# A recommendation network over 200 history items: the loop unrolled, 128-row weights in the head's second layer, three history tiles per l fetched by address

## The chip, the cores and the metric

The kernel runs on one core of a Trainium2 chip. The core's engines run side by side, each through its own list of instructions: TensorE (PE) multiplies matrices, VectorE (DVE) and ScalarE (ACT) work elementwise, GpSimd (POOL) here only starts indirect DMAs, and SyncE (SP) only starts other DMAs. They wait for one another by semaphores. ACT too can start DMAs from its own queue. The metric is the device time of one execution in microseconds (us); lower is better. Times of several runs are given as a median.

## The reference

For each of B = 16384 samples the network looks up a user, an item and a category row, and L = 200 history items. All rows have D = 64 floats. A small attention layer scores each history item against the sample's item, and the history rows are summed with these weights:

```python
u, it, c, h = u_emb[user], i_emb[item], c_emb[cate], i_emb[hist]
feat = concatenate([h, it, h - it, h * it], axis=-1)
a = dice(feat @ au_W1 + au_b1, au_alpha, axis=1)   # statistics over the batch, for each l
w = a @ au_W2 + au_b2
cur = sum(w * h, axis=0)                           # over l
z = concatenate([u, it, c, cur], axis=-1)
z = dice(z @ W1 + b1, alpha1, axis=0)
z = dice(z @ W2 + b2, alpha2, axis=0)
return z @ W3 + b3
# dice(x) = x * (p + alpha * (1 - p)), p = sigmoid((x - mean) * rsqrt(var + 1e-8))
```

The attention layer has 36 hidden values, the three layers of the head 80, 40 and 2. Everything is float32. The bulk of the data is the 200 x 16384 history rows of 256 bytes each, picked at random from a table of some 100,000 rows.

## The kernel before

The batch is cut into 128 tiles of 128 samples, and 16 tiles make a chunk; so each history position l has ND = 8 chunks, and the body is 200 x 8 = 1600 steps of one chunk each. A step k handles several chunks at different stages (lines 421 to 445): it gathers chunk k, turns and multiplies chunk k - 1, adds and measures k - 3, and applies the gate and the weighted sum of chunk k - 10 (LAG), for which the statistics of its whole l must be known. There are 16 row buffers, so gathers may run up to six steps ahead of the weighted sum that frees a buffer.

`fetch` (line 346) starts one indirect DMA on POOL per tile: 128 rows by a list of indices on the partitions. `turn` transposes the rows on DVE and copies the result on ACT; `product` multiplies on PE, with the item's transposed chunk loaded from memory by SP (`load_items`, line 393, three buffers; the load for step k + 1 is issued in step k and waits until DVE's product of k - 2 has read that buffer). `gate` runs on ACT, `weights` and `weigh` on DVE. `moments` closes the statistics of an l in one step of eight.

Some tiles are not gathered by POOL. For the chunks in SIDES, the last tile may come "by address": SP loads the 128 indices into one partition (`addr`), DVE scales them to byte addresses, and then SP or ACT loads them into registers in groups (`TENSOR_LOAD`, line 303) and starts one plain DMA of 256 bytes per row into a `side` or `aside` buffer (lines 314 and 325). In `turn`, ACT copies that buffer into the chunk's rows (line 389). Before, the pattern has a period of four l: SP brings three tiles and ACT two in four l, that is 1.25 of 128 tiles per l. Class `Queue` decides in which step each group is fetched: `when(q)` gives the step, and `lead` and `span` shift and spread it. In a step SP's rows stand ahead of its item load, and ACT's rows stand behind the gate.

The order of all instructions on each engine is the order in which the program writes them. The 192 first l run in a device loop of two turns with 96 l each (lines 503 to 506); the last 8 l and the head follow. Ahead of it, the opening (lines 465 to 501) loads index lists, prepares the attention weights, gathers and turns the items, fills the first addresses, and loads the head's weights.

The head (from line 508) gathers category and user rows for each chunk, runs layer one while the last steps of the body drain, takes the statistics over the batch (`head_moments`: statistics, a small matmul that sums over partitions, deviation, a second matmul, root, reciprocal), and runs layers two and three. Layer one's 80 outputs are split: 64 per half of the samples in `za`, 16 in `zb`, whose four chunks lie on 32 partitions each. Layer two therefore multiplies each half chunk twice, once with the 128-row weights `w2a` and once with the 32-row slice `w2b[q]`:

```python
nc.tensor.matmul(pz[c % 4][:, cols], w2a, cur[c][:, cols], start=True, stop=False)
nc.tensor.matmul(pz[c % 4][:, cols], w2b[q], ab[c // 4][q, cols], start=False, stop=True)
```

A float32 matmul appears in the profile as two passes.

Of the kernel before, what the change touches and what calls it, by code (L numbers as in the profile page):

```python
# [20 lines left out]
LPB = 96  # L21
# [6 lines left out]
SIDES = (5, 6)  # L28
PERIOD = 4
BY_SP = ((1, 5), (2, 5), (3, 5))  # L30
BY_ACT = ((1, 6), (3, 6))
# [5 lines left out]
def din_kernel(  # L37
# [36 lines left out]
    BODY = L - L % LPB if L > LPB else 0  # L74
# [79 lines left out]
    def transpose(dst, of):  # L154
        for i in range(2):
            for e in range(2):
                nc.vector.transpose(by_tile(dst[ts(e, D)], i), of[ts(i, D), :, ts(e, S)])  # L157
# [58 lines left out]
    w2b = make("w2b", P, P)  # L216
# [4 lines left out]
    res = [make(f"res{i}", P, 4, TD, ZO) for i in range(2)]  # L221
# [7 lines left out]
    def head_weights():  # L229
# [8 lines left out]
        for g in range(2):  # L238
# [6 lines left out]
            for j in range(4):  # L245
                r = slice(j * S + g * ZB, j * S + (g + 1) * ZB)
                nc.sync.dma_start(w2b[r, g * ZA : g * ZA + Z2], W2[ZA:])
# [14 lines left out]
    class Queue:  # L262


        def __init__(self, engine, tiles, group, lead, span, buffers, addresses):
            self.engine, self.tiles, self.group, self.lead, self.span = engine, tiles, group, lead, span
            self.buffers, self.addresses, self.n = buffers, addresses, len(buffers)
            self.per = P // group

# [12 lines left out]
        def events(self, k, count):  # L282
            for m in range(count):
                q = m * self.per
                if self.when(q) - 8 == k:
                    yield self.load, m
                if self.when(q) - 5 == k:
                    yield self.scale, m
            for q in range(count * self.per):
                if self.when(q) == k:  # L290
                    yield self.fetch, q

        def load(self, m, l0):
            j = NC + SIDES.index(self.tiles[m % len(self.tiles)][1])
            nc.sync.dma_start(self.addresses[m % self.n], r_hist[ds(l0 + self.line(m), 1), j * P : (j + 1) * P])

        def scale(self, m, l0):
            nc.vector.tensor_scalar_mul(self.addresses[m % self.n], self.addresses[m % self.n], ROW)

        def fetch(self, q, l0):  # L300
# [120 lines left out]
    def step(k, last=None, rows_by_scalar=()):  # L421

        def has(j):
            return last is None or j <= last

        if has(k):
            fetch(k)
# [11 lines left out]
        for q, l0 in rows_by_scalar:  # L439
            by_scalar.fetch(q, l0)  # L440
# [6 lines left out]
    def ask(k, l0, n, more):  # L447
        late = []
        for q in queues:
            per = len(q.tiles)  # L450
            for what, m in q.events(k, n * per // PERIOD + (more and 2)):
                if q is by_scalar and what == q.fetch:
                    late.append((m, l0))
                else:
                    what(m, l0)
        return late

    def steps(l0, n, more):
        for k in range(n * ND):
            l, c = divmod(k, ND)  # L460
            if c == 0 and l + 1 < n + more:
                load_hist_ids((l + 1) % IDX, l0 + l + 1, by_address(l + 1))
            step(k, rows_by_scalar=ask(k, l0, n, more))

    with tc.manual_schedule():
# [6 lines left out]
        for t in (*hT, *xs, *side, *aside, *hm):  # L472
# [3 lines left out]
        for i in range(3):  # L476
            nc.vector.memset(rstds[i], 0.0)
            nc.vector.memset(shifts[i], 0.0)
        nc.vector.bn_stats(stats[-1 % 3][:, 0, :], hm[0][:, :CH])
        for c in range(1, 2 * ND):  # L480
            nc.vector.tensor_copy(stats[-1 % 3][:, c, :], stats[-1 % 3][:, 0, :])
# [12 lines left out]
        for t in px:  # L494
            layer(t, [(blk_m, hm[0])])
        load_items(0)
        for k in range(-16, 0):
            ask(k, 0, L, 0)
        head_weights()
        for t in rows[2:]:  # L500
            nc.vector.memset(t, 0.0)
# [6 lines left out]
    K = (L - BODY) * ND  # L508
# [3 lines left out]
    zb = flat_rows[3:5]  # L512
    pz = [px[K % 2], px[(K + 1) % 2], pg, py]
# [11 lines left out]

    def head_layer(j):
        c, u = divmod(j, 2)
        if u == 0:
            pairs = ((2, ucT[j % 4]), (1, itT[(K + c) % ITEMS]))
        else:  # L530
            transpose(hT[c % TURNED], cur[c].rearrange("p (n d) -> p n d", d=D))
            pairs = ((3, hT[c % TURNED]), (0, ucT[j % 4]))
        layer(pz[0], [(w1a[:, f], t) for f, t in pairs], first=not u, last=u == 1)
        layer(pz[1][:S], [(w1b[:, f], t) for f, t in pairs], first=not u, last=u == 1)
        if u:
            nc.scalar.activation(za[c], pz[0], AF.Identity, bias=b1a)
            measure_head(0, c, za[c])
            nc.scalar.activation(zb[c // 4][ts(c % 4, S)], pz[1][:S], AF.Identity, bias=b1b)
# [3 lines left out]
    with tc.manual_schedule():  # L542
        steps(BODY, L - BODY, 0)
        for j in range(2 * ND + 2):
# [4 lines left out]
            step(K + j, last=K - 1)  # L549
            if 1 <= j <= 2 * ND:  # L550
                transpose(ucT[(j - 1) % 4], spare[(j - 1) % 3])
            if j >= 2:
                head_layer(j - 2)

        def head_moments(i, same):
            mv = small.tile([P, 2], F32, tag=f"hmv{i}", name="hmv")
            nc.vector.bn_aggr(mv, zst[i].rearrange("p c s -> p (c s)"))
            pm = (pg, py)[i % 2]
            nc.tensor.matmul(pm[:, 0:1], same, mv[:, 0:1], start=True, stop=True)
            mean = small.tile([P, 1], F32, tag=f"hmean{i}", name="hmean")  # L560
            nc.vector.tensor_copy(mean, pm[:, 0:1])
            dev = small.tile([P, 1], F32, tag=f"hdev{i}", name="hdev")
            nc.vector.tensor_sub(dev, mv[:, 0:1], mean)
            nc.vector.scalar_tensor_tensor(dev, dev, dev, mv[:, 1:2], ALU.mult, ALU.add)
            nc.tensor.matmul(pm[:, CH : CH + 1], same, dev, start=True, stop=True)  # L565
            rstd = small.tile([P, 1], F32, tag=f"hrstd{i}", name="hrstd")
            shift = small.tile([P, 1], F32, tag=f"hshift{i}", name="hshift")
            scale_and_shift(mean, pm[:, CH : CH + 1], rstd, shift)
            return rstd, shift
# [11 lines left out]
        na, nb = head_moments(0, same_a), head_moments(1, same_b)  # L581
        ab = ucT[:2]
        for j in range(2):
            dice(ab[j], zb[j], nb, al1b, alb)
        for c in range(ND + 1):
            if c < ND:
                dice(cur[c], za[c], na, al1a, ala)
                q = ts(c % 4, S)
                for h in range(2):
                    cols = ts(h, CH)  # L590
                    nc.tensor.matmul(pz[c % 4][:, cols], w2a, cur[c][:, cols], start=True, stop=False)
                    nc.tensor.matmul(pz[c % 4][:, cols], w2b[q], ab[c // 4][q, cols], start=False, stop=True)
            if c:
                nc.scalar.activation(z2[c - 1], pz[(c - 1) % 4], AF.Identity, bias=bias2)
                measure_head(2, c - 1, z2[c - 1])

        n2 = head_moments(2, same_a)
        for c in range(ND):
# [56 lines left out]
```

## Time and profile before

| | us |
|---|---|
| median of 3 runs (32289.11 to 32293.9) | 32292.97 |
| the profiled execution, its own time | 32292.57 |
| its span, first to last instruction | 32290.8 |
| POOL busy | 24281.4 |
| DVE busy | 22882.8 |
| PE busy | 9918.7 |
| ACT busy | 6057.9 |

The page gives the busy time of each engine and then groups of instructions: line, engine, operation, tiles written and read, shape and count; behind the first bar the busy time and the mean length in ns, behind the second the idle time of that engine just before the group's instructions and what ended it. "issue" means that the engine waited for nothing that the profile shows. In the timeline the first column is the start in us, the second the length. PEclk is the clock that TensorE was granted, as a share of full speed. "SPq" and "ACTq" are DMAs issued from these engines' queues.

### The profile page before, as it was taken

The page shows a single profiled execution, that of the slowest core. Times are in us where ns is not written, and L with a number is a line of the kernel's source. Part 1 is how long each engine was busy: PE and PEld are TensorE (multiplying, and loading weights), DVE is VectorE, ACT ScalarE, POOL GpSimd, SP SyncE. Part 2 cuts the span into 40 slices and gives each one's busy share as a digit, 9 for nine tenths or more (in the row PEclk, how much of TensorE's full clock was granted, in tenths as well). Part 3 has the DMA queues.
Part 4 walks back from the last instruction along what each step waited for, and adds up shares of the span by engine and source line. Part 5 has one row for each costly group of instructions (what it writes and reads, how often), then busy time and mean ns, then how long its engine had stood idle before and what let it go on. Part 6 is the DMA issues. An engine that isn't in the chain of part 4 may idle for free.

```text
span 32290.8 us, 175696 instructions
## 1 busy us (share of the span) xinstructions
PE 9918.7 (31%) x13212; PEld 3717.7 (12%) x13212; DVE 22882.8 (71%) x31911; ACT 6057.9 (19%) x5738; POOL 24281.4 (75%) x25739
## 2 busy tenths in 40 slices
PE   2333323333333333233233333333333333333334
PEld 1111111111111111111111111111111111111111
DVE  6777777777777777777677777777777777777775
ACT  1111111111111111111111111111111111111111
POOL 7777777777777777777777777777777777777776
PEclk6666666666666666666666666666666666666666
DMA  2222222222222222222222222222222222222221
GB/s 55 54 54 53 54 54 54 54 54 54 54 54 54 54 54 53 54 54 54 53 54 54 54 53 54 54 54 54 53 54 54 54 54 53 54 54 54 54 53 39
DMA packets 1179260, 1726.19 MB, mean 53 GB/s; under 512 B 559010, under 2 KB 559260, under 8 KB 1177980
## 3 DMA queue, kind: packets, MB, share of 16 engines
q0 software_dynamic: 823488, 844.90, 15.1%
q1 hardware_dynamic: 328604, 866.62, 7.8%
q14 instruction: 1175, 9.63, 0.1%
q10 hardware_dynamic: 25888, 3.33, 0.1%
q8 instruction: 105, 1.72, 0.0%
HBM read 1708.61 MB, written 4.33 MB: 53 GB/s over the span
## 4 chain that ended last, share of the span: by engine, by line
POOL 32%; issue 11%; DMA 4%; DVE 4%; ACT 1%; PE 0%; SPq 0%; DVEq 0%; POOLq 0%; ACTq 0%
POOL rows L128 32%; DMA rows<-in_L_rec_i_emb,idx 4%; DVE hT L157 1%; DVE xs L376 0%; DVE st L381 0%; DVE pg L359 0%; DVE py L358 0%; ACT L354 0%; DVE py L360 0%; DVE py L372 0%; ACT pg L354 0%; ACT pg L355 0%; DVE pg L364 0%; DVE other L408 0%; DVE mv L404 0%
## 5 line engine op out<-in xcount | busy, mean ns | idle before, releaser
L128 POOL DMA_INDIRECT rows<-in_L_rec_i_emb,idx x25350 | 23918.5, 944 | 7749.0 <-issue 7452.1
L162 PE MATMUL px<-hT,blk_h 128*128 128x512 f32 x6404 | 5972.1, 1088 | 21637.1 <-DVE xs L376 21622.7
L157 DVE STREAM_TRANSPOSE hT<-rows 64x512 f32<-64x512 f32 x6404 | 4518.4, 706 | 7674.6 <-DMA rows<-in_L_rec_i_emb,idx 7476.0
L391 ACT COPY py<-hT 128x1024 f32<-128x1024 f32 x1601 | 1627.3, 1016 | 24930.0 <-DVE hT L157 24930.0
L162 PEld LDWEIGHTS px<-hT,blk_h 128*128 128x128 f32 x6404 | 1880.6, 324 | 24758.2 <-DVE xs L376 23104.6
L162 PE MATMUL px<-hm,blk_m 128*128 128x512 f32 x6412 | 3970.5, 752 | 369.2 <-DVE hm L398 368.0
L358 DVE TENSOR_TENSOR py<-pg,xs 128x1024 f32<-128x1024 f32 x1610 | 1985.0, 1233 | 615.7 <-ACT pg L355 468.9
L162 PEld LDWEIGHTS px<-hm,blk_m 128*128 128x128 f32 x6412 | 1757.9, 277 | 3276.1 <-issue 1878.5
L381 DVE BATCH_NORM_STATS2 st<-xs 128x6 f32<-128x512 f32 x3206 | 2062.3, 685 | 55.1
L359 DVE STREAM_TRANSPOSE pg<-py 128x1024 f32<-128x1024 f32 x1610 | 2037.1, 1265 | 55.9
L360 DVE TENSOR_REDUCE py<-pg 128x32 f32<-128x1024 f32 x1610 | 1985.0, 1233 | 54.7
L372 DVE TENSOR_TENSOR py<-rows,pg 128x1024 f32<-128x1024 f32 x1610 | 1978.3, 1229 | 55.2
L373 DVE TENSOR_TENSOR cur<-py,cur 128x1024 f32<-128x1024 f32 x1610 | 1970.7, 1224 | 55.6
L376 DVE TENSOR_TENSOR xs<-px,itp 128x1024 f32<-128x1024 f32 x1603 | 1963.2, 1225 | 50.6
L354 ACT ACTIVATE pg<-xs,sh,rs 128x1024 f32<-128x1024 f32 x1610 | 1937.1, 1203 | 35.3 <-DVE py L372 32.6
L398 DVE TENSOR_TENSOR hm<-py,itT 128x1024 f32<-128x1024 f32 x1601 | 1933.9, 1208 | 0.0
L355 ACT ACTIVATE pg<-pg,au_al,au_1al 128x1024 f32<-128x1024 f32 x1610 | 1895.0, 1177 | 54.2
L364 DVE SCALAR_TENSOR_TENSOR pg<-py,au_bias,part 32x16 f32<-32x16 f32 x6440 | 1538.9, 239 | 227.0
L361 DVE COPY part<-py 64x32 f32<-64x32 f32 x1610 | 312.6, 194 | 55.9
L354 ACT ACT_TABLE_LOAD x204 | 261.7, 1283 | 3.6
L171 ACT ACT_TABLE_LOAD x203 | 260.4, 1283 | 7.5 <-PE pg L565 4.0
L408 DVE COPY other<-mv 32x2 f32<-32x2 f32 x804 | 158.6, 197 | 15.1
(138 smaller groups left out, 1514.0 us busy)
## 6 DMA issues: line engine op xcount, KB each, us to landing
itT<-items SPq DMA_DIRECT2D x1609, 512.0 KB
rows<-in_L_rec_i_emb,idx POOLq DMA_INDIRECT x25350
side<-in_L_rec_i_emb SPq DMA_DIRECT2D x19200, 0.2 KB
aside<-in_L_rec_i_emb ACTq DMA_DIRECT2D x12800, 0.2 KB
idx<-in_r_hist SPq DMA_DIRECT2D x200, 63.0 KB
items<-itT SPq DMA_DIRECT2D x8, 512.0 KB
idx<-in_r_hist SPq DMA_DIRECT2D x150, 0.5 KB
addr<-in_r_hist SPq DMA_DIRECT2D x150, 0.5 KB
```

The lines of the kernel that those rows point to most:

```text
L128: nc.gpsimd.indirect_dma_start(out=dst[:, n, :], out_offset=None, in_=table, in_offset=bass.IndirectOffsetOnAxis(ap=ids, axis=0),)
L157: nc.vector.transpose(by_tile(dst[ts(e, D)], i), of[ts(i, D), :, ts(e, S)])
L162: nc.tensor.matmul(dst[:, ts(i, CH)], lhsT, rhs[:, ts(i, CH)], start=(first and j == 0), stop=(last and j == len(pairs) - 1), skip_group_c ...
L354: nc.scalar.activation(pg, xs[k % XR], AF.Sigmoid, bias=shifts[i], scale=rstds[i])
L358: nc.vector.tensor_mul(py, pg, xs[k % XR])
L359: nc.vector.transpose(pg, py)
L360: nc.vector.reduce_sum(total, pg.rearrange("p (n a) -> p n a", a=S), axis=mybir.AxisListType.X)
L372: nc.vector.tensor_mul(of, rows[k % ROWS], w.unsqueeze(2).to_broadcast([P, TD, D]))
L373: nc.vector.tensor_add(cur[k % ND], py, cur[k % ND])
L376: nc.vector.tensor_add(xs[k % XR], px[k % 2], itp[k % ND])
L381: nc.vector.bn_stats(stats[l % 3][:, 2 * c + i, :], xs[k % XR][:, ts(i, CH)])
L398: nc.vector.tensor_mul(hm[k % 2], py, itT[k % ITEMS])
```

## The change

Six things are changed.

1. The device loop is gone: all 200 l are written out, and the opening's work that only served the loop (clearing hT, xs, hm and the row buffers, a dummy statistic, a dummy product) is gone too.
2. Three tiles of every l come by address and not five in four l: SP brings the last tiles of chunks 1 and 5, ACT that of chunk 6. SP fetches two groups of 16 rows in every step, up to eight steps ahead of the l; ACT two groups of 8, four steps ahead. The first of these are fetched before step 0.
3. The head's weights are loaded ahead of the items, not behind them.
4. Layer two of the head uses four 128-row copies of `w2b`, each with only 32 rows other than zero, on the whole of `ab`.
5. In layer one the product with `cur` moves to the category's half step, and the last user chunk is transposed in two parts, 12 tiles and 4.
6. The moments of the two parts of layer one are taken together; the activation tables are loaded by dummy activations ahead of their use; both answers of layer three come behind all its dices; the output DMAs alternate between SP and ACT.

```diff
-SIDES = (5, 6)
-PERIOD = 4
-BY_SP = ((1, 5), (2, 5), (3, 5))
-BY_ACT = ((1, 6), (3, 6))
+SIDES = (1, 5, 6)
+PERIOD = 1
+BY_SP = ((0, 1), (0, 5))
+BY_ACT = ((0, 6),)
...
-    by_sync = SyncQueue(mybir.EngineType.SP, BY_SP, 16, 2, PERIOD * ND // len(BY_SP), side, addr)
-    by_scalar = ScalarQueue(mybir.EngineType.Activation, BY_ACT, 8, 0, 13, aside, aaddr)
+    by_sync = SyncQueue(mybir.EngineType.SP, BY_SP, 16, 8, 4, side, addr)
+    by_scalar = ScalarQueue(mybir.EngineType.Activation, BY_ACT, 8, 4, 8, aside, aaddr)
...
-        for t in (*hT, *xs, *side, *aside, *hm):
+        for t in (*side, *aside):
             nc.vector.memset(t, 0.0)
         for t in cur:
             nc.vector.memset(t, 0.0)
...
+        head_weights()
...
         load_items(0)
         for k in range(-16, 0):
-            ask(k, 0, L, 0)
-        head_weights()
-        for t in rows[2:]:
-            nc.vector.memset(t, 0.0)
-
-    if BODY:
-        with tc.For_i(0, BODY, LPB) as l0:
-            with tc.manual_schedule():
-                steps(l0, LPB, 1)
+            for q in ask(k):
+                by_scalar.fetch(q)
...
         if u == 0:
-            pairs = ((2, ucT[j % 4]), (1, itT[(K + c) % ITEMS]))
+            transpose(hT[c % TURNED], cur[c].rearrange("p (n d) -> p n d", d=D))
+            pairs = ((2, ucT[j % 4]), (1, itT[(K + c) % ITEMS]), (3, hT[c % TURNED]))
         else:
-            transpose(hT[c % TURNED], cur[c].rearrange("p (n d) -> p n d", d=D))
-            pairs = ((3, hT[c % TURNED]), (0, ucT[j % 4]))
+            pairs = ((0, ucT[j % 4]),)
...
+        for c in range(ND):
+            dice(cur[c], za[c], na, al1a, ala)
+            if c % 4 == 0:
+                dice(ab[c // 4], zb[c // 4], nb, al1b, alb)
+            for h in range(2):
+                cols = ts(h, CH)
+                nc.tensor.matmul(pz[c % 4][:, cols], w2a, cur[c][:, cols], start=True, stop=False)
+                nc.tensor.matmul(pz[c % 4][:, cols], w2b[:, c % 4], ab[c // 4][:, cols], start=False, stop=True)
             if c:
...
+                second(c - 1)
+        second(ND - 1)
...
+        for c in range(ND):
+            g, q = divmod(c, 4)
+            dice(cur[c], z2[c], n2, al12, al2)
+            layer(pz[2 * g], [(w3[:, q], cur[c])], first=q == 0, last=q == 3)
+        for g in range(2):
+            answer(g)
```

More of the change, by code (lines that the diff above doesn't have):

```diff
@@ L215, in din_kernel @@
     w2a = make("w2a", P, P)
-    w2b = make("w2b", P, P)
+    w2b = make("w2b", P, 4, P)
     w3 = make("w3", P, 4, P)
@@ L438, in step @@
             gate(k - LAG)
[L439 to L440 removed]
+        for q in rows_by_scalar:
+            by_scalar.fetch(q)
         if has(k - 1):
@@ L445, in step, with ask @@
             weigh(k - LAG)
-    def ask(k, l0, n, more):
+    def ask(k):
         late = []
         for q in queues:
-            per = len(q.tiles)
-            for what, m in q.events(k, n * per // PERIOD + (more and 2)):
+            for what, m in q.events(k, L * len(q.tiles) // PERIOD):
                 if q is by_scalar and what == q.fetch:
-                    late.append((m, l0))
+                    late.append(m)
                 else:
-                    what(m, l0)
+                    what(m)
         return late
[L458 to L463, printed above, removed]
     with tc.manual_schedule():
@@ L512, in din_kernel @@
     zb = flat_rows[3:5]
+    res = [
+        flat_rows[2][:, i * 4 * TD * ZO : (i + 1) * 4 * TD * ZO].rearrange("p (i n o) -> p i n o", i=4, n=TD)
+        for i in range(2)
+    ]
     pz = [px[K % 2], px[(K + 1) % 2], pg, py]
@@ L542, in din_kernel @@
     with tc.manual_schedule():
-        steps(BODY, L - BODY, 0)
+        for k in range(K):
+            step(k)
         for j in range(2 * ND + 2):
@@ L548, in din_kernel @@
                     load_items(K + j // 2)
-            step(K + j, last=K - 1)
+            step(K + j)
+            if 2 <= j and j % 2 == 0:
+                head_layer(j - 2)
             if 1 <= j <= 2 * ND:
-                transpose(ucT[(j - 1) % 4], spare[(j - 1) % 3])
-            if j >= 2:
+                head_turn(j - 1)
+            if 2 <= j and j % 2 == 1:
                 head_layer(j - 2)
[L555 to L569, printed above, removed]
```

122 lines of the change are left out of this document (69 added, 53 removed).

## The prediction

> **What bounds it.** I read the page's busy shares first, then the costliest groups, then the waits of POOL, DVE, SP and ACT, then the timeline at both ends and stretches of the head. Page and groups:
>
> ```profile
> span 32290.8 us, 175696 instructions
> PE 9918.7 (31%) x13212; PEld 3717.7 (12%) x13212; DVE 22882.8 (71%) x31911; ACT 6057.9 (19%) x5738; POOL 24281.4 (75%) x25739
> L128 POOL DMA_INDIRECT rows<-in_L_rec_i_emb,idx x25350 | 23918.5, 944 | 7749.0 <-issue 7452.1 <-DMA rows<-in_L_rec_i_emb,idx 226.3 <-DVE py L372 44.5
> ```
>
> Waits of POOL and DVE (total us, times, longest us):
>
> ```profile
> POOL rows L128 <- issue: 7562.4, 24770, 11.1
> POOL rows L128 <- DVE rows L501: 7.1, 1, 7.1
> POOL rows L128 <- DMA addr<-in_r_hist: 3.2, 1, 3.2
> DVE hT L157 <- DMA rows<-in_L_rec_i_emb,idx: 7476.0, 1464, 6.7
> ```
>
> POOL is 75% busy, yet it is the bound. Its 25,350 hist gathers take 0.944 us each and stand 0.30 us apart, and that gap is "issue": nothing else is waited for. Only three gaps are longer: 11.1, 7.1 and 3.2 us, at the loop's entry, turn and exit. Without them one gather costs (23918.5 + 7749.0 - 21.4 + 0.9) / 25350 = 1.2484 us. DVE, which consumes the rows, waits for gathers 7476 us, 4.7 us in each of the 1600 steps; its work is 22882.8 / 1600 = 14.3 us a step against 20.2. So the body's time is the number of gathers times 1.2484, and only the two ends, where POOL stalls or has finished, add to it.
>
> **Gathers moved.** Before, 250 of 25,600 hist tiles go by address (five in four l); after, 600 (three per l). POOL loses 350 gathers: 350 x 1.2484 = -436.9 us, all on the bounding path. A step then takes 15.625 x 1.2484 = 19.5 us. What takes the rows over must fit into it. From the lines' own views, the timeline and SP's waits:
>
> ```profile
> L303 ACTq TENSOR_LOAD <-aaddr x102: 712/722/877, 10007.6 to 11986.4; - x102
> L303 SPq TENSOR_LOAD <-addr x76: 1154/1168/1277, 10009.5 to 11968.8; - x76
> L325 ACTq DMA_DIRECT2D aside<-in_L_rec_i_emb x816: 222/222/488, 10008.4 to 11989.7; - x164
> 15016.62 5.17 SPq L314 DMA_DIRECT2D side<-in_L_rec_i_emb  x16
> SPq L314 <- DMA side<-in_L_rec_i_emb: 134.1, 394, 0.7
> 15014.11 0.35 SPq L394 DMA_DIRECT2D itT<-items  x1
> L389 ACT COPY rows<-side 128x64 f32<-128x64 f32 x150 | 35.5, 236 | 134.7 <-issue 134.7
> ```
>
> SP: two groups of 16 rows a step, each one register load of 1.17 and 5.17 of issues: 2 x 6.34 = 12.7, the item load 0.35, and four small loads per l (index list, three address lists, 0.36 each, 0.2 a step): 13.2 us of 19.5. Waits for landing added 134.1 us over 19,200 rows, 0.1 a group. The item load of the next step stands behind these rows on SP; it is issued two steps before DVE's product needs it, so 13.2 us of delay is covered; if the rows took over 19.5 us, that cover would be gone and SP would set the step (a rival below). ACT: two groups of 8 a step, each 0.72 + 8 x 0.31 = 3.2 to 3.5, so 7 us behind the gate's two activations. With ACT's own 6057.9 / 1600 = 3.8 us that is 10.8 of 19.5, and the next work queued on ACT, the copy of hT, comes only with the next step's gathers. 350 more copies of a side tile (0.24 us on ACT) and 350 scalings of one row of addresses on DVE (at 1 us each still 0.2 a step) fall into idle time of about 9 and 4.7 us a step. I cost all this at nothing.
>
> **Loop removed.** The three gaps lose what exceeds 0.30: 21.4 - 0.9 = -20.5 us. The body was straight-line code of 96 l already and POOL kept its period in it, so unrolling further adds nothing that a row shows. Bounds: 0 (if an equal wait takes its place) to -20.5; I take -20.5, as none of the three causes is left.
>
> **Opening.** The head's weights are now loaded before the items are turned. Timeline:
>
> ```profile
> 15.59 0.91 DVE L473 MEMSET hT<- 128x1024 f32 x1 [0.16 <-issue]
> 28.85 0.91 DVE L475 MEMSET cur<- 128x1024 f32 x1 [0.16 <-issue]
> 39.08 2.87 DVE L157 STREAM_TRANSPOSE itT<-rows 64x512 f32<-64x512 f32 x4
> 43.17 0.94 POOL L128 DMA_INDIRECT rows<-in_L_rec_i_emb,ids  x1 [0.30 <-issue]
> 173.43 12.17 SPq L314 DMA_DIRECT2D side<-in_L_rec_i_emb  x32
> 185.70 0.34 SPq L236 DMA_DIRECT2D w1a<-in_L_rec_W  x1
> 208.15 0.23 DVE L258 TENSOR_SCALAR same_b<-same_b 128x128 f32<-128x128 f32 x1
> ```
>
> DVE ends the attention weights at 15.6; side and aside take 0.6, the eight cur memsets 8 x (0.91 + 0.16) = 8.6, w1a's memset 0.5: SP may load w1a from about 25.4. From SP's first weight load to the end of same_b it took 208.38 - 185.70 = 22.7 us, and DVE waits through it. So the first item transposes start at 48.1, not 39.08, and end at 51.0. POOL's gather 33 reuses that buffer and would stand at 43.17: a stall of 51.2 - 43.17 = +8.0 us, once; later tiles come every 20 us.
>
> Then SP fetches 256 rows ahead of step 0: eight times 12.17 + 1.17 = 107 us from about 181 to 288, and step 0's 32 rows to 302. The index list of l = 1 and the item load for product 1 stand behind them. POOL reaches l = 1 at 171 + 125 x 1.2484 = 327: 25 us of slack. DVE's product 1 runs at about 308 instead of 210; at 14.3 a step it has weighed step 0 by 308 + 8 x 14.3 + 15 = 437, and POOL needs that row buffer, the sixteenth, at 171 + 250 x 1.2484 = 483. Cost 0, slack 25 us. Should a group take 8.1 us here and not 6.7, this cover is gone, and each us beyond is paid.
>
> **Head.** Behind the last gather (ends 32149.9) come 140.9 us without POOL:
>
> ```profile
> 32148.92 0.94 POOL L128 DMA_INDIRECT rows<-in_L_rec_u_emb,ids  x1 [0.30 <-issue]
> 32151.68 2.92 DVE L157 STREAM_TRANSPOSE itp<-rows 64x512 f32<-64x512 f32 x4 [7.21 <-DMA rows<-in_L_rec_u_emb,ids]
> 32156.12 1.12 PE L162 MATMUL px<-hT,w1a 128*128 128x512 f32 x2 [3.39 <-DVE hT L157]
> 32165.11 1.10 ACT L538 ACTIVATE rows<-px,b1b 32x1024 f32<-32x1024 f32 x1 [2.44 <-PE px L162]
> 32166.24 1.28 DVE L518 BATCH_NORM_STATS2 zst<-rows 128x6 f32<-128x512 f32 x2 [2.25 <-ACT rows L538]
> 32174.80 2.37 ACT L576 ACTIVATE hm<-rows,hshift,hrstd 128x1024 f32<-128x1024 f32 x2
> 32188.25 2.07 PE L592 MATMUL px<-itp,w2b 32*128 32x512 f32 x2
> 32190.25 2.08 PE L591 MATMUL px<-cur,w2a 128*128 128x512 f32 x2
> 32247.60 1.28 DVE L518 BATCH_NORM_STATS2 zst<-rows 128x6 f32<-128x512 f32 x2 [6.73 <-ACT rows L594]
> 32251.58 1.28 ACT L171 ACT_TABLE_LOAD   x1 [4.01 <-PE pg L565]
> 32254.90 2.37 ACT L576 ACTIVATE hm<-rows,hshift,hrstd 128x1024 f32<-128x1024 f32 x2
> 32269.52 0.81 DVE L577 TENSOR_SCALAR rows<-rows,al,al 128x1024 f32<-128x1024 f32 x1
> 32270.37 1.23 DVE L578 TENSOR_TENSOR cur<-rows,rows 128x1024 f32<-128x1024 f32 x1
> 32282.78 0.36 DVE L607 TENSOR_TENSOR res<-xs,bias 128x64 f32<-128x64 f32 x2
> ```
>
> Last tile of layer one: last gather's end to the end of the last statistics, 32167.5 - 32149.9 = 17.7 us. hT's transpose (2.9) and half of the matmuls (8.9 us for eight, now four) are done earlier, and only a quarter of the last transpose is left (0.95). 1.8 landing + 0.95 + PE 5.6 (half of 8.9, with a slow start taken dear) + ACT 1.1 + DVE 1.3 + 0.2 = 10.9: -6.8.
> Moments: 7.3 us, two chains in a row and a table load; now one chain for both, the Sigmoid table loaded beside DVE's last two steps: 5.7: -1.6. The second moments, 6.0 us (32248.9 to 32254.9), lose the Sqrt load of 1.28 and some of the other, gain a short DVE step: -1.4.
> Layer two: 74.1 us from the first sigmoid to the last statistics. Its 32 matmuls start 2.00 us apart. Stretches of the timeline, PEclk after PE, PEld, DVE, ACT and POOL, and weight loads of layer three:
>
> ```profile
> 32182.00:32246.00 64.00, 63.73 (x64) 15.98 (x64) 22.70 (x29) 14.56 (x13) 0.00 (x0) 0.50 0.00 0
> 32264.00:32268.00 4.00, 3.92 (x10) 1.42 (x8) 0.24 (x2) 0.06 (x1) 0.00 (x0) 1.00 0.00 0
> 32258.30 9.62 PE L162 MATMUL px<-cur,w 128*128 128x512 f32 x16 [6.80 <-DVE cur L578]
> 32264.33 0.19 PEld L162 LDWEIGHTS px<-cur,w 128*128 128x128 f32 x1 [0.24 <-issue]
> 32264.76 0.19 PEld L162 LDWEIGHTS px<-cur,w 128*128 128x128 f32 x1 [0.24 <-issue]
> ```
>
> PE was busy 63.73 of 64.00 us with a granted clock of 0.50 throughout. Layer three, all 128x128, starts slow too, but the clock is 1.00 within 6 us, and passes are then 0.43 us apart, a matmul (two passes) 0.86. With 128-row weights layer two has layer three's shape. Bounds: 32 x 1.71 (the slow half of layer three's 9.62) and 32 x 0.86. I take the fast end after 5.3 us, since that row has the same shapes. Then PE (3.4 a tile) is no longer alone: a tile's loop is PE 3.4, ACT's bias 1.1 and next sigmoid 1.2, DVE's dice 2.0 and one statistics 1.3 of the other tile, 9.0 for two tiles. 5.2 to the first matmul, 7 x 4.5, 3.4 for the last tile, 2.4 behind it: 42.5. -31.4; at the slow clock 61, -13.
> Layer three: 28.2 us to the last result. The first half's transpose and additions stood between the fourth and fifth dice, so the fifth began only at 32269.5; four dice of 0.81 + 1.23, 1.99 apart, reach it by 32264.1. Now all eight run first, 1.2 + 8 x 1.99 = 17.1, PE ends at 19 to 20, then two answers of 1.7: 21.9. -6.4. The output DMAs behind it: 7.65 us, now three and not four issues deep per queue: -0.3, though the first half's stand just ahead.
> Head: -6.8 - 1.6 - 1.4 - 31.4 - 6.4 - 0.3 = -47.9.
>
> By the Trainium skill's page "TensorE: Matmul & The Clock Gate", section "What's actually happening", the clock opens after about 3.4 us of sustained busyness; the 64 busy us at 0.50 contradict that here, layer three's stretch agrees roughly, and the measurement decides. The same page of the Trainium skill, section "Why this matters for your kernels", says that one matmul of 32 weight rows takes the time of one of 128; by that the exchange gives nothing, and the sum would be 31,827.
>
> **Sum.** -436.9 - 20.5 + 8.0 - 47.9 = -497.3, from the profiled execution's 32292.57 us (span 32290.8): 31,795. The median, 32292.97, is 0.4 higher; I say 31,796.
>
> **Rivals.**
> A. Layer two stays at the slow clock, or oscillates: 31,796 + 18 = 31,814. For it: 64 busy us at 0.50 before, and gaps of waits in the new loop. Against: layer three. Chance 0.15.
> B. Layer two keeps 2.00 us a matmul, its pace having another cause: 31,796 + 31 = 31,827. For it: the 128-row matmuls there were as slow as the 32-row ones. Chance 0.08.
> C. SP's 288 rows ahead of the first item loads outlast their cover and POOL stalls in the first 16 steps: 10 to 40 us, 31,821 in the middle. For it: 25 us is not much. Chance 0.08.
> D. Gathers grow slower as 48 rows a step share the DMA engines, and the gain is given back: within 0.2% of before if the period grows by 17 ns, to 1.266. Against: 0.944 and 0.30 stood through stretches with and without rows. Time 32,290, chance 0.02.
> E. SP becomes the bound: with 0.60 us a row (landings twice as late, with few rows in flight) a group costs 10.8 and a step 22.1, 1600 x 22.1 + 280 = 35,600. It decides against the change from 20.2 us a step, 0.54 a row; the row measured is 0.32, waits of at most 0.7 seen. Chance 0.04.
>
> **Numbers.** Forecast as summed: 0.63. A to C are faster too, so faster has 0.94, within 0.2% (about what a measurement of this kernel tells from none) 0.02, slower 0.04. The range holds the forecast, A, B and most of C: from 31,775 (opening stall gone, layer two at PE's 28 us) to 31,838.
>
> **What would show it.** POOL at 25,000 hist gathers with the period still near 1.248 and no gap over 0.3 us but one near 43 us; SP's item loads still waiting for DVE's hm most of each step; about 93 us from the last gather to the end; PEclk near 1.00 in layer two. It is wrong if POOL waits for DVE or an index list, or DVE for item loads, in the body.

## The result, and the profile after

The changed kernel takes 31,800.34 us (median; 31,799.17 to 31,801.48), the kernel before 32,292.96 beside it. The ratio is 0.9848 with a 95% interval of 0.9836 to 0.9859: 492.6 us or 1.5% faster. The forecast was 31,796.

The page of the changed kernel, with the same rows as for the kernel before:

```profile
span 31799.3 us, 270304 instructions
PE 9881.5 (31%) x13196; PEld 3707.9 (12%) x13196; DVE 22816.1 (72%) x32088; ACT 6126.3 (19%) x6061; POOL 23955.0 (75%) x25389
L126 POOL DMA_INDIRECT rows<-in_L_rec_i_emb,idx x25000 | 23592.1, 944 | 7625.2 <-issue 7297.1
```

Its waits by engine (total us, times, longest us):

```profile
POOL rows L126 <- issue: 7408.0, 24289, 0.3
POOL rows L126 <- DVE itT L155: 9.3, 1, 9.3
SPq L392 <- DVE hm L396: 7403.9, 1381, 21.5
DVE hT L155 <- DMA rows<-in_L_rec_i_emb,idx: 6913.2, 1459, 12.2
```

POOL still starts one gather behind the other. All its waits in the body are at most 0.3 us, and the three long ones at the loop's entry, turn and exit are gone; the 9.3 us lie in the opening, ahead of the body. DVE still waits for gathers 6913 us, 4.3 us a step, so nothing behind POOL has become the bound. SP still waits 7404 us for DVE to free an item buffer: its 51,200 rows, where it had 19,200, fit into the step.

The period is (23592.1 + 7625.2) / 25000 = 1.24869 us, where it was 1.24840. This third of a nanosecond is the only thing in the body that was not forecast, and over 25,000 gathers it is +7.2 us.

The opening, by the timeline (start us, length us). The first two rows are the stall of POOL's gather 33 behind DVE's first item transposes, the others the end of SP's 288 rows, the loads queued behind them, and DVE's product 1, which waits for the item load:

```profile
48.88 5.79 DVE L155 STREAM_TRANSPOSE itT<-rows 64x512 f32<-64x512 f32 x8
52.03 0.94 POOL L126 DMA_INDIRECT rows<-in_L_rec_i_emb,ids  x1 [9.34 <-DVE itT L155]
...
289.42 11.62 SPq L312 DMA_DIRECT2D side<-in_L_rec_i_emb  x32
301.09 0.37 SPq L139 DMA_DIRECT2D idx<-in_r_hist  x1
301.56 0.39 SPq L392 DMA_DIRECT2D itT<-items  x1
305.55 1.23 DVE L396 TENSOR_TENSOR hm<-py,itT 128x1024 f32<-128x1024 f32 x1 [55.49 <-DMA itT<-items]
```

The head, by the timeline: the last gather, the last statistics of layer one, the first sigmoid of layer two, its last statistics, the first sigmoid of layer three, the last result and the last output DMA. Then stretches of layer two (us, then busy time of PE, PEld, DVE, ACT and POOL, then the granted clock of PE):

```profile
31707.59 0.94 POOL L126 DMA_INDIRECT rows<-in_L_rec_u_emb,ids  x1 [0.30 <-issue]
31718.02 1.28 DVE L503 BATCH_NORM_STATS2 zst<-rows 128x6 f32<-128x512 f32 x2 [0.97 <-ACT rows L531]
31723.62 1.23 ACT L587 ACTIVATE hm<-xs,hshift,hrstd 128x1024 f32<-128x1024 f32 x1
31764.62 1.29 DVE L503 BATCH_NORM_STATS2 zst<-rows 128x6 f32<-128x512 f32 x2 [2.76 <-ACT rows L597]
31770.43 2.36 ACT L587 ACTIVATE hm<-rows,hshift,hrstd 128x1024 f32<-128x1024 f32 x2
31791.01 0.36 DVE L619 TENSOR_TENSOR rows<-xs,bias 128x64 f32<-128x64 f32 x2
31794.89 0.32 SPq L628 DMA_DIRECT2D out<-rows  x1
```

```profile
31727.10:31732.50 5.40, 5.40 (x6) 1.98 (x7) 3.75 (x4) 0.01 (x1) 0.00 (x0) 0.50 0.00 0
31732.50:31763.40 30.90, 26.60 (x59) 10.25 (x57) 22.50 (x28) 15.70 (x14) 0.00 (x0) 1.00 0.00 0
```

From the last gather's end (31708.5) to the end (31799.3) pass 90.8 us, where it was 140.9. In layer two PE runs 5.4 us at half its clock and then the whole of the rest at 1.00.

### The profile page after: what moved, and what is told of

It is laid out like the page before. It is cut to its first block, busy times and chain, and to the rows that moved or that the text cites. A ratio compares the mean times of both kernels' runs of the same rounds, so it can differ in the third digit from the quotient of the medians.

```text
span 31799.3 us, 270304 instructions
## 1 busy us (share of the span) xinstructions
PE 9881.5 (31%) x13196; PEld 3707.9 (12%) x13196; DVE 22816.1 (72%) x32088; ACT 6126.3 (19%) x6061; POOL 23955.0 (75%) x25389
## 4 chain that ended last, share of the span: by engine, by line
POOL 59%; issue 22%; DMA 9%; DVE 7%; ACT 2%; SPq 1%; PE 0%; ACTq 0%; DVEq 0%; POOLq 0%
POOL rows L126 59%; DMA rows<-in_L_rec_i_emb,idx 9%; DVE hT L155 2%; DVE xs L374 1%; DVE st L379 1%; DVE pg L357 1%; ACT L352 1%; DVE py L358 1%; DVE py L356 1%; DVE py L370 1%; ACT pg L352 1%; ACT pg L353 1%; DVE pg L362 0%; DVE other L406 0%; SPq L312 0%
## 5 line engine op out<-in xcount | busy, mean ns | idle before, releaser
L126 POOL DMA_INDIRECT rows<-in_L_rec_i_emb,idx x25000 | 23592.1, 944 | 7625.2 <-issue 7297.1
L387 ACT COPY rows<-side 128x64 f32<-128x64 f32 x400 | 97.7, 244 | 2573.1 <-DMA side<-in_L_rec_i_emb 2559.8
```

The lines of the kernel that those rows point to most:

```text
L126: nc.gpsimd.indirect_dma_start(out=dst[:, n, :], out_offset=None, in_=table, in_offset=bass.IndirectOffsetOnAxis(ap=ids, axis=0),)
```

## The experiments

In the first group of runs the kernel before took 32,290.72 us. The second and third groups fell on another chip, on which it took 38,355.66 and 38,300.77 us; their times stand against these alone.

**The gathers: the old pattern in the new kernel.** One part undone: five tiles in four l by address, as before; no loop and the new head stay.

```diff
-SIDES = (1, 5, 6)
-PERIOD = 1
+SIDES = (5, 6)
+PERIOD = 4          # and BY_SP, BY_ACT, lead and span as before
```

> The changed kernel with the by-address pattern of before (five tiles in four l, with the old lead and span), and all else as changed. Theory (the body's time is the number of gathers times the gather's own time): 350 gathers come back, +436.9 us at 1.2484 us each, and the gather's period goes back from 1.2487 towards 1.2484 us, -7 us; the opening's 288 rows on SP shrink as well, which should cost or bring nothing, because they were covered. So about 32,230 us, and the last gather's end moves by about +430 us while the head behind it stays at 91 us. If instead the loop's removal or the head's order were what made the body faster, the time would stay near 31,800. If the period does not fall back, the theory that row DMAs lengthen it is wrong, and the time is near 32,237.

Measured: 32,229.73 us, ratio 0.9981 (0.9972 to 0.9991). Its group of gathers:

```profile
L126 POOL DMA_INDIRECT rows<-in_L_rec_i_emb,idx x25350 | 23918.5, 944 | 7728.7 <-issue 7477.6
```

This is a period of 1.24841 us, that of before. So the loop, the opening and the head together are worth 61.0 us (32,290.7 - 32,229.7), and the 350 moved gathers 429.4 (to 31,800.3), or 431.6 if each time is set against the kernel before in its own group (492.6 - 61.0): 350 x 1.2484 = 436.9, less the 7 us of the longer period. The longer period goes with the rows. In the changed kernel's trace, gathers between whose starts no row was issued are 1248.4 ns apart, with rows of SP alone 1248.7, with rows of ACT 1248.9.

**Layer two: 32-row weights back.** Only the second product of layer two is changed.

```diff
-nc.tensor.matmul(pz[c % 4][:, cols], w2b[:, c % 4], ab[c // 4][:, cols], start=False, stop=True)
+nc.tensor.matmul(pz[c % 4][:, cols], w2b[ts(c % 4, S), c % 4], ab[c // 4][ts(c % 4, S), cols], start=False, stop=True)
```

> The changed kernel with the 32-row slice of the weights in layer two again, all else as changed. Theory (the 32-row weights keep PE's clock at 0.50, and their alternation with 128-row weights costs about 0.3 us a matmul): 32 matmuls 2.00 us apart, granted clock 0.50 for 64 us, layer two again about 71 to 74 us from the first sigmoid to the last statistics instead of 42.3, the whole 29 to 32 us longer than the changed kernel, about 31,830 us. Rival (it was the order of the dices or the single bias step that shortened layer two): the stage stays near 42 us and the whole near 31,800.

Measured: 31,826.16 us, ratio 0.9856 (0.9840 to 0.9873). A stretch over all of layer two:

```profile
31722.60:31787.00 64.40, 64.14 (x64) 15.97 (x64) 26.44 (x32) 15.92 (x16) 0.00 (x0) 0.50 0.00 0
```

and two of its first matmuls in the timeline:

```profile
31724.66 2.07 PE L607 MATMUL px<-itp,w2b 32*128 32x512 f32 x2
31726.66 2.08 PE L606 MATMUL px<-cur,w2a 128*128 128x512 f32 x2
```

The old pace is back: 2.00 us from matmul to matmul, busy throughout, the clock at 0.50. From the first sigmoid to the last statistics layer two takes 70.1 us (31719.2 to 31789.3), against 42.3 in the changed kernel and 74.1 before. So the weights alone are worth 27.8 us of the 31.8 gained there, and the new order around them 4.0. The medians differ by 25.8 us, and by 28.1 when each is set against the kernel before in its own group.

**Layer two: 32-row weights, grouped.** The same weights, but per tile first both 128-row products, then both 32-row ones. Two theories: 32-row matmuls keep the clock down as such, or the change of height at every matmul does.

```diff
-                nc.tensor.matmul(pz[c % 4][:, cols], w2b[:, c % 4], ab[c // 4][:, cols], start=False, stop=True)
+            for h in range(2):
+                cols = ts(h, CH)
+                nc.tensor.matmul(pz[c % 4][:, cols], w2b[ts(c % 4, S), c % 4], ab[c // 4][ts(c % 4, S), cols], start=False, stop=True)
```

> As the run with 32-row slices, but in each tile both 128-row matmuls come first and both 32-row matmuls behind them, so that the height of the weights changes half as often. Theory one (a 32-row matmul does not count as enough activity, so the clock stays at 0.50 whatever the order; the switch between heights costs its own 0.3 us): clock 0.50, mean distance of matmuls about 1.85 us, layer two about 67 us, the whole about 31,825 us. Theory two (the switch itself interrupts the activity that opens the clock): with pairs the clock opens for part of the time, matmuls come down towards 0.9 us and layer two to 45 to 60 us, the whole 31,803 to 31,818 us.

Measured: 31,804.85 us, ratio 0.9849 (0.9833 to 0.9866). Stretches of its layer two:

```profile
31723.50:31727.20 3.70, 3.66 (x4) 1.17 (x4) 3.63 (x4) 0.05 (x1) 0.00 (x0) 0.50 0.00 0
31727.20:31734.00 6.80, 6.23 (x13) 2.21 (x12) 3.34 (x5) 2.77 (x3) 0.00 (x0) 0.94 0.00 0
31734.00:31740.70 6.70, 6.60 (x8) 1.99 (x8) 3.28 (x5) 1.71 (x2) 0.00 (x0) 0.57 0.00 0
```

a shorter closed stretch further on and the open one behind it:

```profile
31751.97:31755.38 3.41, 3.41 (x5) 0.97 (x4) 3.04 (x4) 0.90 (x1) 0.00 (x0) 0.50 0.00 0
31755.38:31762.21 6.83, 6.06 (x14) 2.20 (x13) 3.50 (x5) 3.36 (x3) 0.00 (x0) 1.00 0.00 0
```

and matmuls of both in the timeline:

```profile
31723.54 3.75 PE L606 MATMUL px<-cur,w2a 128*128 128x512 f32 x4 [5.20 <-ACT rows L587]
31727.22 2.38 PE L609 MATMUL px<-itp,w2b 32*128 32x512 f32 x4
31729.53 1.98 PE L606 MATMUL px<-cur,w2a 128*128 128x512 f32 x4
...
31734.10 3.03 PE L606 MATMUL pg<-cur,w2a 128*128 128x512 f32 x4 [0.67 <-DVE cur L589]
31737.07 3.78 PE L609 MATMUL pg<-itp,w2b 32*128 32x512 f32 x4
...
31751.36 3.17 PE L606 MATMUL px<-cur,w2a 128*128 128x512 f32 x4 [0.77 <-DVE cur L589]
31754.46 2.42 PE L609 MATMUL px<-itp,w2b 32*128 32x512 f32 x4
```

The clock opens and closes again and again. Four passes take 1.98 us where it is open and 3.75 where not, whichever the height. So 32-row matmuls do not bar the clock by standing in the loop. Four full-height passes in a row, 3.75 us at the half clock, were enough to open it; two in a row, 2.0 us, never were with the 32-row weights back in turn. The trace shows more than that. From 31728.07 on, the clock is open for 6.83 us, closed for 10.24, open for 6.83, closed for 3.41 and open for 6.83 again. All of these are multiples of 3.41 us, so it changes on a grid in time. In the 3.41 us before the three openings full-height passes ran for 2.6, 2.8 and 2.5 us, the 32-row ones for the rest; in the other closed stretches they ran for at most 2.2 us.

**Layer two: 64 rows, and 32 rows alone.** Two runs on the other chip, read by layer two only. The first takes 64-row slices in the second product. The second leaves the 128-row product out and does the 32-row one twice, so part of layer two is not computed.

```diff
-nc.tensor.matmul(pz[c % 4][:, cols], w2b[:, c % 4], ab[c // 4][:, cols], start=False, stop=True)
+nc.tensor.matmul(pz[c % 4][:, cols], w2b[ts(c % 4 // 2, 2 * S), c % 4], ab[c // 4][ts(c % 4 // 2, 2 * S), cols], start=False, stop=True)
```

```diff
-nc.tensor.matmul(pz[c % 4][:, cols], w2a, cur[c][:, cols], start=True, stop=False)
+nc.tensor.matmul(pz[c % 4][:, cols], w2b[ts(c % 4, S), c % 4], ab[c // 4][ts(c % 4, S), cols], start=True, stop=False)
-nc.tensor.matmul(pz[c % 4][:, cols], w2b[:, c % 4], ab[c // 4][:, cols], start=False, stop=True)
+nc.tensor.matmul(pz[c % 4][:, cols], w2b[ts(c % 4, S), c % 4], ab[c // 4][ts(c % 4, S), cols], start=False, stop=True)
```

> The changed kernel with 64-row slices of the second weights in layer two, alternating with 128-row weights at every matmul as the 32-row slices did. Theory (the change of the weights' height at every matmul costs 0.15 us a switch and keeps the clock shut, whatever the height): matmuls 2.0 us apart, clock 0.50, the whole 31,824 to 31,828 us like the 32-row run. Rival (what counts is how many weight rows work, and 64 and 128 in turn are enough): the clock opens after 5 to 6 us, layer two takes 42 to 48 us, the whole 31,800 to 31,806 us.

> Layer two with 32-row weights alone: the product with the 128-row weights is left out, and the 32-row product is done twice in its place, so the number of matmuls is the same and the height never changes (the place of the 32 rows changes once per tile). This leaves out part of layer two, so the output is not the reference's. Theory (switching of height keeps the clock shut): no switch, so the clock opens after 5 to 6 us and matmuls come 0.86 us apart; layer two about 42 us, the whole about 31,800 us. Rival (32 rows are too little activity): clock 0.50 throughout, matmuls 1.71 us apart, layer two about 61 us, the whole about 31,818 us.

Stretches over layer two, first of the kernel with 64 rows:

```profile
47912.80:47977.00 64.20, 64.14 (x64) 15.94 (x64) 26.34 (x32) 15.72 (x16) 0.00 (x0) 0.50 0.00 0
```

then of the kernel with 32 rows alone:

```profile
47906.10:47945.00 38.90, 35.80 (x64) 15.95 (x64) 24.34 (x30) 15.72 (x15) 0.00 (x0) 0.50 0.00 0
```

and some of its matmuls in the timeline:

```profile
47909.69 2.08 PE L606 MATMUL px<-itp,w2b 32*128 32x512 f32 x4
...
47914.12 1.06 PE L606 MATMUL px<-itp,w2b 32*128 32x512 f32 x1
47914.29 1.06 PE L606 MATMUL pg<-itp,w2b 32*128 32x512 f32 x1
```

128 rows in turn with 64 behave as in turn with 32: 2.00 us a matmul, clock 0.50 for 64 us. With 32 rows alone no height changes at all, and yet the clock stays at 0.50 for 38.9 us. So the change of height alone does not explain it either. What fits all six kernels, the one before and the changed one with them, is that the clock follows passes of full height only: 2.5 us of them or more in one 3.41 us of the grid opened it, 2.2 us or less did not. With 32 or 64 rows in turn no such stretch holds more than 2.0 us of them, and lower passes alone did not open it. This is an inference from layer two alone; which signal the clock follows was not measured. The number of weight rows at work, averaged over a stretch, is a rival that these runs hardly part from it: 102 of 128 rows at the least before an opening, up to 102 in turn with 64 rows and no opening. By the Trainium skill's page "TensorE: Matmul & The Clock Gate", section "What's actually happening", about 3.4 us of sustained busyness open the clock. The runs agree with this length, but only if passes of 32 and 64 rows do not count as busy, or not fully, which the page does not say.

The last two rows show one thing more. Two tiles' passes start 0.17 us apart and run side by side, so 64 passes fit into 38.9 us even at the slow clock. The Trainium skill's page "TensorE: Matmul & The Clock Gate", section "Why this matters for your kernels", says that products in different slices of 32 rows run at the same time; this trace agrees.

**The opening: DVE's steps moved.** In the changed kernel DVE waits for SP's weight loads before it turns the first items. The short steps that need these loads go into a function of their own behind the items.

```diff
+    def head_scales():           # al1a, al1b, al12, same_a, same_b, out of head_weights
...
         load_items(0)
+        head_scales()
```

> The changed kernel with the head's weight loads still early, but the nine DVE steps that wait for these loads (one minus alpha three times, the two averaging matrices) moved behind the item transposes. Theory (POOL's stall of 9.3 us at the 33rd gather comes from DVE waiting for the loads before it turns the first items): the stall is gone, the last gather ends 9 us earlier, the whole 31,791 us. Rival (the later work has slack that the stall did not touch, or the rows that SP fetches ahead of step 0 then bind): the stall goes, but POOL waits elsewhere in the first 16 steps and less than 5 us is won.

Measured: 31,789.69 us, ratio 0.9845 (0.9828 to 0.9861), the fastest of all and 10.65 us ahead of the changed kernel, or 8.4 when each is set against the kernel before in its own group (501.0 and 492.6 us gained). Its timeline at the place of the stall:

```profile
44.64 2.88 DVE L155 STREAM_TRANSPOSE itT<-rows 64x512 f32<-64x512 f32 x4 [14.86 <-DMA rows<-in_L_rec_i_emb,ids]
49.23 0.94 POOL L126 DMA_INDIRECT rows<-in_L_rec_i_emb,ids  x1 [0.30 <-issue]
```

DVE now waits for rows instead of weights, and POOL has no gap left. The two spans differ by 12.7 us (31799.3 to 31786.6): 9.0 for the stall, 3.3 for the period, 1.24856 us in this run and 1.24869 in that, and 0.4 for the end. So the stall was paid in full. The rows are the same in both kernels, so the 3.3 us are a difference between two traces that nothing here explains.

**More tiles by address.** Four and four and a half tiles of each l, on top of that version, each in two runs on the other chip. The diff is that of four tiles; with four and a half ACT brings two per l. The rows' spans and the lead of SP's rows and of the address loads are shortened to fit. The second pair of texts is for the same two kernels again.

```diff
-SIDES = (1, 5, 6)
-PERIOD = 1
-BY_SP = ((0, 1), (0, 5))
-BY_ACT = ((0, 6),)
+SIDES = (1, 3, 5, 6)
+PERIOD = 2
+BY_SP = ((0, 1), (0, 5), (1, 1), (1, 3), (1, 5))
+BY_ACT = ((0, 3), (0, 6), (1, 6))
```

> The version with the moved DVE steps of the opening, and four tiles of each l by address instead of three: SP brings five tiles in two l (2.5 groups of 16 rows a step), ACT three (three groups of 8 a step); loads of addresses and leads adapted, the same number of buffers. Theory (POOL's count of gathers is the time as long as SP and ACT fit into a step): 200 gathers fewer, 200 x 1.2487 = -250 us against the run with the moved DVE steps, about 31,540 us; SP about 17.2 and ACT about 14.4 of 19.4 us a step; the gather's period at most 1.2490. Rival (SP's slack is too small where three groups fall into one step, or ACT's rows push back the copy of the next turned chunk): item loads come late, DVE waits for them in the body, POOL waits for DVE, and the time lies above 31,600 us.

> As the run with four tiles, but nine tiles in two l: SP again five, ACT four (four groups of 8 rows in every step). Theory: 300 gathers fewer than with three tiles, 31,790 - 375 = about 31,416 us, if ACT fits: four groups of 3.54 us and 3.9 us of its own are 18.1 us of a step of 19.3. Rival (ACT becomes the bound, since its rows stand between the gate of one step and the copy of the next, and the statistics step once in an l takes DVE 19.5 us with ACT waiting in it): more than 19.3 us a step, time 31,450 us or above, POOL waiting for DVE or ACT in the body; from 19.9 us a step on it would be slower than three tiles.

> The version with the DVE steps moved (31,789.7) and with four tiles of each l by address in place of three, two and a half on SP, one and a half on ACT. On a chip on which the kernel before takes 32,291: theory (POOL): 200 gathers less, 31,789.7 - 249.7 = 31,540, for SP has 40 rows a step at 0.42 us (2.5 groups of 6.70 us = 16.8 of 19.35 us) and ACT 24 (3 groups of 3.62 us = 10.9, and 3.8 us of its other work). Rival (SP or ACT cannot keep up, since a wait holds up the rows behind it): over 31,790. On a chip on which the kernel before takes 38,356: 51,000 as there measured before.

> As the version with four tiles, with two on ACT instead of one and a half. On a chip on which the kernel before takes 32,291: theory (POOL): 100 gathers less again, 31,540 - 124.9 = 31,415. Rival: ACT has 32 rows a step (4 groups of 3.62 us = 14.5) and 3.8 us of other work, 18.3 of 19.3 us, so that its waits no longer fit and DVE waits for it: over 31,540. On a chip on which the kernel before takes 38,356: 52,400 as there measured before.

Measured: 50,997.19 and 51,016.36 us for four, ratios 1.3298 and 1.3312; 52,360.91 and 52,361.12 for four and a half, ratios 1.3654 and 1.3670. The kernel with 64 rows, which has the change's three tiles, takes 48,009.34 there, ratio 1.2514 (1.2494 to 1.2535). So on this chip the body of the change makes the kernel 25% slower, and each further tile makes it slower still. Whether more than three tiles pay where the kernel before takes 32,291 stays untried. The waits of the kernel with 64 rows:

```profile
POOL rows L126 <- DVE py L370: 14365.0, 712, 22.5
DVE hm L396 <- DMA itT<-items: 15948.3, 800, 87.6
SPq L392 <- DVE hm L396: 50.6, 3, 19.1
```

Some of SP's rows in its timeline (start and length in us, count at the end), first a whole step's 32 and then 12 of a slow stretch, and below them rows of the changed kernel on its own chip:

```profile
16008.77 11.64 SPq L312 DMA_DIRECT2D side<-in_L_rec_i_emb  x32
...
16028.04 31.49 SPq L312 DMA_DIRECT2D side<-in_L_rec_i_emb  x12
```

```profile
16008.80 12.49 SPq L312 DMA_DIRECT2D side<-in_L_rec_i_emb  x32
```

Twelve rows take 31.5 us where 32 took 12.5. SP no longer waits for DVE; DVE waits for the item load queued behind SP's rows, up to 87.6 us, and POOL waits for DVE. That is the chain of waits of rival E in the prediction, at a mean step of 30.0 us (48,009 / 1600). But E has every row dearer, and here they are slow in stretches only: of the 3,200 groups of 16 rows half took under 5.5 us from the first start to the last, as 90% do on the other chip, and a quarter over 19. DVE is held up by the item load in 800 of the 1600 steps.

**What is slow on that chip: no rows, and rows of SP alone.** Two kernels, one with all 25,600 tiles gathered by POOL, one with two tiles of each l on SP and none on ACT.

```diff
+SIDES = ()            # BY_SP = (), BY_ACT = (), queues = ()
...
+SIDES = (1, 5)        # BY_SP = ((0, 1), (0, 5)), BY_ACT = (), queues = (by_sync,)
```

> The changed kernel with no row by address: all 25,600 gathers of the history on POOL (200 x 8 x 16), SP and ACT issue no row. On a chip on which the kernel before takes 32,291: theory (POOL's count of gathers sets the time): 600 gathers more than in the changed kernel at 1.2484 us are +749.0, and the period falls back from 1.24869 to 1.2484 (25,000 x 0.00029 = -7), so 31,800.3 + 749.0 - 7.3 = 32,542. On a chip on which the kernel before takes 38,356: if the rows issued by SP and ACT are the whole of what is slow there, this kernel comes to 32,540 to 32,600 there too, and so ahead of the kernel before; if the chip is slow for another reason (gathers, memory), it stays above 38,000.

> The changed kernel with two tiles of each l by address, both on SP, and none on ACT. On a chip on which the kernel before takes 32,291: 200 gathers more than in the changed kernel, 31,800.3 + 200 x 1.2484 = 32,050. On a chip on which the kernel before takes 38,356: theory one (every row issued costs the same there; the kernel before loses 6,064 us over 32,000 rows, 0.19 us a row, and the changed kernel with a 64-row second product 16,212 us over 76,800, 0.21 us a row): 32,050 + 51,200 x 0.20 = 42,300. Theory two (only rows of SP and ACT at the same time as POOL's gathers get in each other's way): 32,050 to 34,000.

Measured: 36,850.16 us without rows, ratio 0.9619 (0.9603 to 0.9635); 47,510.39 with rows of SP alone, ratio 1.2401 (1.2380 to 1.2422). Neither pair of theories holds. Without rows the kernel is some 4,300 us above the 32,542 worked out for the other chip, so the rows are not the whole. With rows of SP alone it is 15,460 above 32,050, 0.30 us for each of 51,200 rows, so it is neither a fixed 0.20 a row nor a matter of SP and ACT together. These 0.30 us are an average: here too half of the groups of 16 rows took under 5.5 us. A group of DVE in the kernel without rows:

```profile
L362 DVE SCALAR_TENSOR_TENSOR pg<-py,au_bias,part 32x16 f32<-32x16 f32 x6400 | 1530.1, 239 | 4033.7 <-issue 3479.7
```

its waits:

```profile
DVE pg L362 <- issue: 3479.7, 2959, 1.9
POOL rows L126 <- DVE py L370: 4196.1, 370, 20.2
```

and the same group in the changed kernel on its own chip:

```profile
L362 DVE SCALAR_TENSOR_TENSOR pg<-py,au_bias,part 32x16 f32<-32x16 f32 x6400 | 1529.4, 239 | 225.6
```

The short instructions take 239 ns on both. On the slow chip DVE stands 3,480 us before them with nothing to wait for, and by this and the like before other groups DVE is late for POOL: the 4,196 us that POOL waits are nearly all of the 4,300.

## Why the prediction was right, point by point

**What bounds it.** Right: POOL's count of gathers times its period. The old pattern alone moves some 430 of the 492 us.

**Gathers moved.** -436.9 forecast, -429.7 in the profile (25,350 x 1.24840 less 25,000 x 1.24869). The count was right. The period rose by 0.29 ns; rival D, gathers that grow slower, named this direction, but its point of decision, 17 ns, is 60 times as far.

**SP, ACT and DVE at nothing.** Right on this chip: SP still waits 7,404 us for DVE, ACT's rows end in time, no wait of POOL in the body is over 0.3 us. The row price of 0.32 us that spoke against rival E held on the chip that the trace came from; on the other one it fails in every second step or so, and E's chain of waits decides.

**Loop removed.** -20.5 forecast; the three gaps are gone and nothing took their place.

**Opening.** +8.0 forecast, +9.0 measured: the first transposes start at 48.9 instead of 48.1. The run with the moved steps confirms it. SP's rows ahead of step 0 ended at 301.0 (forecast 302), product 1 came at 305.5 (308), and POOL did not stall: rival C did not occur, and the cover of 25 us stood as worked out. The 210 us given there for product 1 before are too early, since DVE still cleared row buffers until 223.4; nothing rests on them. ACT's own rows ahead of step 0 were in no term: they held product 0 back by 36.7 us, which the same cover took up.

**Head.** -47.9 forecast, -50.1 measured (140.9 to 90.8). By parts, forecast and measured: last tile of layer one 10.9 and 10.8; first moments 5.7 and 4.3; layer two 42.5 and 42.3; second moments 4.6 and 4.5; layer three 21.9 and 20.9; output 7.35 and 7.9, since SP issued the last output DMA only at 31794.9. The first moments were mis-sized most, -3.0 instead of -1.6, then layer three, -7.3 instead of -6.4. Two differences of the recorded sum are slips: 74.1 less 42.5 is 31.6, not 31.4, and 28.2 less 21.9 is 6.3, not 6.4; together they are 0.1 us. Rivals A and B did not occur: the clock opened after 5.4 us (5.3 forecast) and stayed open, matmuls 0.86 us apart. Two hits in layer two are partly luck. Layer three of the changed kernel opened the clock after 3.0 us, so 5.3 was one draw from the grid. And the 42.3 us are two misses that cancel: the first tile's products, most of them at half the clock, ended 10.0 us behind the first sigmoid and not 8.6 (5.2 + 3.4), and the seven other tiles took 29.9 us and not 31.5.

**Sum.** The measured terms give -429.7 - 20.5 + 9.0 - 50.1 = -491.3; the spans differ by 491.5. Against the forecast's -497.3 the terms are 6.0 short: +7.2 for the period and +1.0 for the stall, less 2.2 in the head. Between forecast and median 4.3 us remain.

## What to carry to other kernels

Where one engine starts equal work back to back and all others wait for it, count what is moved off it and multiply by its period; here this came within 2%. Then ask how much of the new carrier's step is filled: 13.2 of 19.5 us was safe while a row cost 0.32 us, and the same plan lost 25% where it did not, so a slack that hangs on one price deserves a second chip. Where TensorE runs at half its clock, try full-height weights back to back; here 3.0 to 5.4 us of them opened it, and filling three quarters of a weight block with zero rows cost nothing here.

## What the runs showed of the hardware that was not expected

The same kernel takes very different times on two chips, the one before 32,291 and 38,356 us, and kernels with three tiles by address, alike but for layer two, take about 31,800 and 48,009: the change gains on one and loses on the other. On the slow chip gathers keep their 1.249 us wherever POOL is not waiting. But in stretches of some 30 us, instructions of SP, ACT and POOL begin one by one in steps of 0.70 or 1.40 us. Counted over all starts of SP in the trace, 6,725 of 111,523 instructions of the kernel with 64 rows follow the one before by 0.70 us, to within 0.02, and 15,740 by 1.40, against 38 and 9 in the changed kernel on its own chip. Without rows it is DVE, with 6,631 instructions at 1.40 us against 47. What holds them back does not show in the trace, and it stays open, as does whether it is the chip itself or something at work beside it, and whether the unrolled code plays a part: the one kernel with a device loop was not profiled there.

The period of the gathers goes with what other engines issue: it is 0.3 to 0.5 ns longer than 1248.4 in the gathers of the changed kernel that have rows beside them. Another 0.13 ns lie between two kernels with the same rows (1.24869 and 1.24856 us), and what makes these stays open.
